# A graph layer's edge lists compacted in two parts, the first part ahead of the loop and the second inside it

## The chip, the cores and the metric

The kernel runs on one core of one Trainium2 chip. The metric is the device time of one execution in microseconds (us), the median of the runs of one kernel.

## The reference

The layer takes 6250 nodes of 128 features and 206250 edges sorted by destination. What it computes is this:

```python
h = relu(layernorm(x))                       # (6250, 128)
x_i, x_j = h[dst], h[src]
msg = concat([x_i, x_j - x_i], -1) @ W.T + b # per edge
out = segment_max(msg, dst, 6250)
x = x + where(isfinite(out), out, 0)
```

The message splits into a part of the destination (At, taken out of the maximum and added at the end) and a part of the source (Bt = h times the right half of W). So for each node the kernel needs the maximum of Bt rows over its edges.

## The kernel before

**Nodes and edges.** Each of the 128 partitions owns 49 destination nodes, and a window of 1792 edges (`WIN`) that holds all of them. Sources are split as 50 blocks of 125 (`q16` is the block, `swin - 125 * q16` the place in it). Two ways lead from an edge to the maximum:

- the **pair loop** handles, for every destination and every source block, at most one edge. For 13 tiles of up to 10 partitions (`tiles`) and 25 pairs of source blocks each (325 turns of the loop, `pairs`), the tensor engine spreads the chosen places (L739), the scalar engine makes a one-hot of them (L740), two matmul passes multiply it with Bt (L808), and the vector engine takes the maximum into `acc2` (L812, at the end of a tile L829).
- the **stream** handles the edges that are second or later of their (destination, block) cell. Each partition has a list of up to 512 (`REST`) of them. For every list position, GpSimd gathers one Bt row per partition by an indirect DMA (L98, 8 rows to a group, 6 group buffers `rows`), the vector engine runs a segmented maximum over it (L163), and a full group is stored to `M` (L167). A group buffer is free for the next gathers when its store has ended. Behind the last store, 49 gathers (`extract`, L98 again) fetch the row where each node's run ends.

**Everything is ordered by hand** (a manual schedule): each engine runs its instructions in the order in which the lines are reached. `due(k)` says how many stream rows are done after turn k of the loop.

**Before the loop** come, interleaved:

1. 27 `step()` calls: normalize, relu, weigh by W, store Bt and At (L547 to L584, on ACT, PE and SP). The gathers need all of Bt.
2. 46 tests (`shift`, `deep`, `off`, L491 to L505): for each edge, whether one of the 43 edges ahead of it in its run is in the same cell. The vector engine compares all 1792 columns, and the tensor engine adds the answers up in PSUM (`count`, L486).
3. `first` and `res` (L648 to L652): which edges go to the loop, which to the list.
4. Compaction of `res` to the front of each partition: a prefix sum (L666), packing (L675 to L678), and 11 `move`s, each a mask and a predicated copy over up to 1791 columns (L522, L523). `spread` makes from it the gather indices `ridx`, the destinations `sdl` and the limits `slim` (L526 to L534).
5. The first tile's one-hots (`onehots(0)`: `OHQ` by L203, its two end rows set by GpSimd in L200; `OHD` by L208), and its `products` (L246 to L262), from which the loop's first turn starts.

Of the kernel before, what the change touches and what calls it, by code (L numbers as in the profile page):

```python
# [29 lines left out]
F32 = mybir.dt.float32  # L30
# [20 lines left out]
REST = 512  # L51
SH = 43
# [10 lines left out]
def gnn_kernel(tc, x, src, dst, W, b, out):  # L63
# [23 lines left out]
    LASTD = N - (P - 1) * LD  # L87
    SPLIT = ((0, L // 16 * 16), (L // 16 * 16, L))
# [12 lines left out]
    with ExitStack() as ctx:  # L101
# [10 lines left out]
        with ExitStack() as body:  # L112
# [16 lines left out]
            ridx = keep.tile([P, REST], I32, name="ridx")  # L129
# [15 lines left out]
            def gather_group():  # L145
                i = state["gathered"]
                state["gathered"] = i + 1
                G = rows.tile([P, U, C], F32, name="G")
                Gt[i] = G
                for j in range(U):  # L150
                    k = i * U + j
                    gather(G[:, j], Bt[:, :], ridx[:, k:k + 1])
# [114 lines left out]
            with ExitStack() as pre:  # L267
# [68 lines left out]
                junk = pool.tile([P, WIN], BF16, name="junk")  # L336
# [8 lines left out]
                dwin = pool.tile([P, WIN], I32, name="dwin")  # L345
# [8 lines left out]

                kk = pool.tile([P, REST], F32, name="kk")

# [15 lines left out]
                def scales_a(g):  # L372
                    A_.activation(rstd[:, group(g)], mv[:, group(g), 1], AF.Sqrt, bias=eps)
# [29 lines left out]
                qa = pool.tile([P, W2], F32, name="qa")  # L403
# [38 lines left out]
                G_.iota(kk, pattern=[[1, REST]], base=1, channel_multiplier=0, allow_small_or_imprecise_dtypes=True)  # L442
# [35 lines left out]
                first = pool.tile([P, W2], BF16, name="first")  # L478
                val = pool.tile([P, W2], BF16, name="val")
                csum = pool.tile([P, W2], F16, name="csum")  # L480
                nres = pool.tile([P, 1], F32, name="nres")

                def count(e, s):
                    for c0 in range(0, W2, 512):
                        c1 = min(c0 + 512, W2)
                        T_.matmul(dup[:, c0:c1], identb, e[:, c0:c1], start=s == 1, stop=s == SH + 3)  # L486

                def shift(s):
                    e = work.tile([P, W2], BF16, name="eq")
                    i1 = KB[:, 65 - s:65 - s + W2] if s % 2 else KA[:, 64 - s:64 - s + W2]  # L490
                    V.tensor_tensor(e, KA[:, 64:], i1, ALU.is_equal)  # L491
                    count(e, s)

                def deep():

                    s = SH + 1
                    e = work.tile([P, W2], BF16, name="eq")
                    V.memset(e[:, :s], 0.0)
                    V.tensor_tensor(e[:, s:], dlc[:, s:], dlc[:, :W2 - s], ALU.is_equal)
                    count(e, s)  # L500

                def off(j, bound, op, s):

                    e = work.tile([P, W2], BF16, name="eq")
                    V.scalar_tensor_tensor(e, dlc, adj[:, j:j + 1], bound, op0=ALU.add, op1=op)  # L505
                    count(e, s)
# [13 lines left out]
                def move(i):  # L520
                    n = W2 - (1 << i)
                    V.tensor_scalar(sh_[:, :n], pk[:, 1 << i:], 1 << (19 + i), None, op0=ALU.bitwise_and)  # L522
                    V.copy_predicated(pk[:, :n], sh_[:, :n], pk[:, 1 << i:])  # L523

                def spread():
                    V.tensor_scalar(ridx, pk[:, :REST], 8191, None, op0=ALU.bitwise_and)  # L526
                    V.tensor_scalar(nres, csum[:, W2 - 1:W2], -1.0, float(W2), op0=ALU.mult, op1=ALU.add)
                    V.tensor_scalar(sh_[:, :REST], pk[:, :REST], 13, 63, op0=ALU.logical_shift_right,
                                    op1=ALU.bitwise_and)
                    V.tensor_scalar(kk, kk, nres, 63.0, op0=ALU.is_gt, op1=ALU.mult)  # L530
                    V.tensor_tensor(sdl, sh_[:, :REST], kk, ALU.max)
                    s = slim[:, 1:NS]
                    V.tensor_tensor(s, sdl[:, 1:NS], sdl[:, :NS - 1], ALU.is_equal)
                    V.tensor_scalar(s, s, -0.5, FMAX, op0=ALU.add, op1=ALU.mult)  # L534
# [3 lines left out]
                lw = ln.enter_context(tc.tile_pool(name="lw", bufs=2))  # L538
                st = {}
# [72 lines left out]
                for _ in range(6):  # L612
                    step()
# [11 lines left out]

                early = [(s, t, b0) for s, t in ((q16, TQ), (dlc, TD)) for b0 in range(0, NBLK, 4)]
                tests = [lambda s=s: shift(s) for s in range(1, SH + 1)]
                tests += [deep, lambda: off(0, LOb, ALU.is_lt, SH + 2), lambda: off(1, HIb, ALU.is_gt, SH + 3)]
                for n, f in enumerate(tests):
                    f()  # L630
                    if n in (4, 8):
                        load_x(5 + n // 8, (nc.sync, nc.sync))
                    if n % 8 == 5:
                        step()
                    elif n % 5 == 2 and early:
                        turned(*early.pop(0))
                    if n in (16, 32):
                        moments(3 + n // 32)
                        scales_a(3 + n // 32)
                    if n in (18, 34):  # L640
                        scales_b(3 + n // 32)
                assert not early
                cmp_.close()
                hots.append(hotx.enter_context(tc.tile_pool(name="hot0", bufs=1, side="right", reuse_waits="tile")))
                signs, vals = onehots(0)
# [5 lines left out]
                V.scalar_tensor_tensor(first, dup, 0.0, val, op0=ALU.is_equal, op1=ALU.mult)  # L651
                V.tensor_tensor(res, val, first, ALU.subtract)  # L652
                V.scalar_tensor_tensor(qa, q16, float(-L), swin, op0=ALU.mult, op1=ALU.add)
                V.scalar_tensor_tensor(val, qa, float(-L), first, op0=ALU.add, op1=ALU.mult)
                for n in range(2):
                    for f in signs[n * 12:n * 12 + 12]:
                        f()
                    step()
                for b0 in range(0, NBLK, 4):
                    turned(val, TV, b0)  # L660
                for g in (5, 6):
                    moments(g)
                    scales_a(g)

                V.tensor_scalar(first, res, -1.0, 1.0, op0=ALU.mult, op1=ALU.add)
                V.tensor_tensor_scan(csum, first, first, 0.0, op0=ALU.add, op1=ALU.max)  # L666
                for g in (5, 6):
                    scales_b(g)

                f_ = first[:, 1:]  # L670
                V.scalar_tensor_tensor(f_, dlf[:, 1:], 1.0, dlf[:, :WIN - 1], op0=ALU.mult, op1=ALU.is_lt,
                                       accum_out=badc[:, 0:1])
                V.scalar_tensor_tensor(f_, dlf[:, 1:], -1.0, dlf[:, :WIN - 1], op0=ALU.add, op1=ALU.is_gt,
                                       accum_out=badc[:, 2:3])
                V.scalar_tensor_tensor(pk, dlc, 8192.0, swin, op0=ALU.mult, op1=ALU.add)  # L675
                V.tensor_tensor(sh_, csum, res, ALU.mult)
                V.tensor_scalar(sh_, sh_, 19, None, op0=ALU.logical_shift_left)
                V.tensor_tensor(pk, pk, sh_, ALU.bitwise_or)  # L678
                for n in range(2):
                    for f in signs[24 + n * 13:37 + n * 13]:  # L680
                        f()
                    step()
# [3 lines left out]
                mats, rest = products(0, lambda: bank0)  # L686
                for f in mats:
                    f()
                for i in range(11):
                    move(i)  # L690
                    if made["ln"] < NH + 2:
                        step()
                    if 3 <= i < 7:
                        rest[i - 3]()
                while made["ln"] < NH + 2:
                    step()
                spread()
                ln.close()
                while state["gathered"] < 2:
                    gather_group()  # L700


                V.tensor_scalar(badc[:, 1:2], nres, float(REST), None, op0=ALU.is_gt)
# [17 lines left out]
            with ExitStack() as main:  # L721
                accp = main.enter_context(tc.tile_pool(name="accp", bufs=1, reuse_waits="tile"))
                acc = accp.tile([P, P * LD], F32, name="acc")
# [48 lines left out]
                def due(k):  # L772

                    return min(NS, int(2.05 * min(k, NP_) + 1.6 * max(k - NP_, 0)))
# [5 lines left out]
                for k, (t, i) in enumerate(pairs):  # L780
# [28 lines left out]
                    if i == 0:  # L809
                        V.tensor_copy(acc2[:, :, :n], ps[:, :, :n])  # L810
                    else:
                        V.tensor_tensor(acc2[:, :, :n], acc2[:, :, :n], ps[:, :, :n], ALU.max)  # L812
                    while state["ran"] < due(k + 1):
                        if state["gathered"] < NG and state["ran"] >= (state["gathered"] - GB + 1) * U:
                            gather_group()
                        stream_step()
# [122 lines left out]
```

## Time and profile before

| | |
|---|---|
| median of 10 runs (lowest, highest) | 920.14 us (917.55, 921.86) |
| the profiled execution, its own time | 922.75 us |
| its span, first to last instruction | 921.0 us |
| first gather of a Bt row | 180.28 us into the span |
| first turn of the loop reaches `acc2` (L810) | 181.12 us |
| first turn of tile 1, of tile 12 (L810) | 248.59 us, 810.26 us |
| last gather of a Bt row issued | 834.63 us |
| first and last gather from M | 844.53 us, 910.34 us |

Times inside the execution are counted from the start of the span; 1.75 us of the profiled time lie outside it. Busy time of an engine does not count its waits, register work and DMA issue.

### The profile page before, as it was taken

Reading aid. Unit: us, or ns where it says so; the run is one execution under the profiler, and the core shown is the slowest. Engines: PE = TensorE matmul, PEld = TensorE weight load, DVE = VectorE, ACT = ScalarE, POOL = GpSimd, SP = SyncE. Lnnn points to the kernel's source line nnn. Section 1 sums busy time; section 2 is a strip of 40 time slices with the busy share of each in tenths; the row PEclk is TensorE's granted clock in tenths of the full one; section 3 lists DMA queues with packets and bytes.
Section 4 is the critical chain, followed back from the end, with each engine's and each line's share of the span. In section 5 each row is a group of like instructions: output and inputs, shape, how many; then the busy total and the mean of one; then the engine's idle time right before and its main releaser. Section 6 shows DMA issues by size and latency. Waiting matters only on the chain.

```text
span 921.0 us, 14085 instructions
## 1 busy us (share of the span) xinstructions
PE 733.8 (80%) x4272; PEld 511.1 (55%) x4277; DVE 758.9 (82%) x1796; ACT 637.7 (69%) x1623; POOL 567.8 (62%) x638
## 2 busy tenths in 40 slices
PE   1799669868898989999989988999898979849310
PEld 0344345446576666766666666666666657637210
DVE  6689989688898988998989888998889898849532
ACT  0532665788897978998997989899888774626000
POOL 3400000177777777777777777777777777764774
PEclk9999755778999998999999999999999998978655
DMA  4760111322333333333333333333333323374532
GB/s 87 196 151 23 33 35 45 85 98 98 101 118 101 98 98 113 105 100 104 117 98 98 109 112 97 100 118 101 98 98 119 102 94 100 121 202 155 154 94 85
DMA packets 50455, 95.74 MB, mean 104 GB/s; under 512 B 12093, under 2 KB 31254, under 8 KB 50017
## 3 DMA queue, kind: packets, MB, share of 16 engines
q1 hardware_dynamic: 30628, 52.46, 17.1%
q0 software_dynamic: 18736, 41.84, 16.4%
q10 hardware_dynamic: 1009, 0.49, 0.3%
q8 instruction: 34, 0.56, 0.2%
q14 instruction: 48, 0.39, 0.1%
HBM read 50.05 MB, written 44.64 MB: 103 GB/s over the span
## 4 chain that ended last, share of the span: by engine, by line
POOL 26%; DMA 26%; PE 14%; DVE 14%; issue 14%; ACT 5%; POOLq 0%; ACTq 0%; DVEq 0%
POOL G L98 26%; DMA G<-Bt,ridx 23%; PE pm L562 4%; PE ps L808 3%; DVE acc L812 3%; DVE G L163 2%; DVE OHD L208 2%; PE dup L486 2%; DVE eq L491 2%; PE z L739 2%; DMA G<-M,last_e 2%; ACT oh L740 1%; PE pt L552 1%; ACT OHQ L203 1%; DVE stats L365 1%
## 5 line engine op out<-in xcount | busy, mean ns | idle before, releaser
L98 POOL DMA_INDIRECT G<-Bt,ridx x512 | 494.7, 966 | 238.8 <-issue 135.2
L808 PE MATMUL ps<-oh,Bp 126*128 126x490 f32 (+1 forms) x1300 | 409.0, 439 | 44.4 <-DVE acc L812 33.2
L740 ACT ACTIVATE oh<-z 126x490 fp32r<-126x490 f32 (+1 forms) x650 | 339.8, 584 | 116.9 <-PE z L739 115.8
L812 DVE TENSOR_TENSOR acc<-acc,ps 128x980 f32<-128x980 f32 (+1 forms) x312 | 359.7, 1153 | 18.1 <-PE ps L808 16.2
L808 PEld LDWEIGHTS ps<-oh,Bp 126*128 126x128 f32 x1300 | 252.0, 201 | 138.0 <-DVE acc L812 72.7
L163 DVE SCALAR_TENSOR_TENSOR G<-G,slim 128x128 f32<-128x128 f32 x511 | 177.8, 348 | 71.2 <-DMA G<-Bt,ridx 60.5
L739 PE MATMUL z<-Vf,Sel 114*126 114x490 f16 (+1 forms) x650 | 207.9, 394 | 26.2 <-ACT Vf L262 17.6
L203 ACT ACTIVATE OHQ<-TQ,sbias 128x140 bf16<-128x140 bf16 (+1 forms) x637 | 220.5, 428 | 0.0
L246 PEld LDWEIGHTS <-OHQ 128*51 128x51 bf16 x1792 | 96.8, 184 | 50.1 <-issue 49.8
L739 PEld LDWEIGHTS <-Sel 114*126 114x126 f16 x650 | 81.7, 141 | 46.4 <-issue 23.3
L246 PE MATMUL pv<-OHD,OHQ 128*51 128x13 bf16 (+5 forms) x1638 | 101.3, 241 | 3.8 <-DVE OHD L208 3.2
L208 DVE SCALAR_TENSOR_TENSOR OHD<-TD,TV 128x30 bf16<-128x30 bf16 (+5 forms) x637 | 87.9, 184 | 0.0
L98 POOL DMA_INDIRECT G<-M,last_e x48 | 51.2, 1066 | 23.3 <-issue 12.8
L562 PE MATMUL pm<-wT,hT 128*125 128x256 f32 x100 | 48.2, 583 | 20.2 <-ACT hT L556 20.2
L486 PE MATMUL dup<-eq,identb 128*128 128x512 bf16 (+1 forms) x179 | 40.6, 361 | 5.6 <-DVE eq L491 2.4
L863 PE MATMUL pf<-ident,acc 128*128 128x128 f32 x49 | 12.8, 431 | 33.7 <-DVE o L864 32.0
L562 PEld LDWEIGHTS pm<-wT,hT 128*125 128x125 f32 x100 | 23.1, 280 | 28.0 <-ACT hT L556 26.5
L749 ACT ACTIVATE dump<-sdl,nbias 128x512 bf16<-128x512 f32 x50 | 36.8, 736 | 0.1
L864 DVE TENSOR_TENSOR o<-G,pf 128x512 f32<-128x512 f32 x12 | 8.2, 687 | 33.1 <-DMA G<-M,last_e 33.1
L572 ACT CAST Bp<-pm 125x256 fp32r<-125x256 f32 x50 | 18.5, 370 | 23.0 <-PE pm L576 22.1
L200 POOL MEMSET OHQ<- 128x140 bf16 x4 | 0.8, 228 | 53.5 <-PE dup L486 53.5
L486 PEld LDWEIGHTS <-identb 128*128 128x128 bf16 x184 | 18.2, 100 | 23.9 <-issue 9.1
(199 smaller groups left out, 445.4 us busy)
## 6 DMA issues: line engine op xcount, KB each, us to landing
M<-G SPq DMA_DIRECT2D x64, 512.0 KB, 2.8
G<-Bt,ridx POOLq DMA_INDIRECT x512, 2.5
xa<-At SPq DMA_DIRECT2D x1, 2744.0 KB
G<-in_x SPq DMA_DIRECT2D x6, 448.0 KB, 4.4
Bt<-ba SPq DMA_DIRECT2D x12, 224.0 KB, 6.0
At<-ba SPq DMA_DIRECT2D x12, 224.0 KB, 2.9
xo<-in_x SPq DMA_DIRECT2D x3, 728.0 KB, 5.2
out_x<-o SPq DMA_DIRECT2D x3, 512.0 KB, 3.6
```

Source lines behind the costliest of these rows:

```text
L98: G_.indirect_dma_start(out=o, out_offset=None, in_=table, in_offset=bass.IndirectOffsetOnAxis(ap=idx, axis=0))
L163: V.scalar_tensor_tensor(G[:, j], state["prev"], slim[:, k:k + 1], G[:, j], op0=ALU.min, op1=ALU.max)
L203: A_.activation(oq[:, a, :, :nl], TQ[:, :, ls], AF.Sign, scale=2.0, bias=sbias[:, a:a + 1])
L208: V.scalar_tensor_tensor(o[:, bs_, :nl], TD[:, bs_, ls], float(d + 1), TV[:, bs_, ls], op0=ALU.is_equal, op1=ALU.mult)
L246: T_.matmul(o, oq[:, :, b_, l], r, start=k == 0 and b_ == 0, stop=b_ == NBLK - 1, skip_group_check=True)
L486: T_.matmul(dup[:, c0:c1], identb, e[:, c0:c1], start=s == 1, stop=s == SH + 3)
L562: T_.matmul(pm[:L, j], st["hT", i][:, j, :L], wT, start=j == 0, stop=False, skip_group_check=True)
L739: T_.matmul(z[:, :n], Sel[:, i + j], Vf[t % 2][:, :n], start=True, stop=True)
L740: A_.activation(oh[:, j, :n], z[:, :n], AF.Relu)
L749: A_.activation(dump, sdl, AF.Sign, scale=2.0, bias=nbias[:, c:c + 1], accum_out=ends[:, c:c + 1])
L808: T_.matmul(ps[:, j, :n], Bp[:, e, i + j], oh[:, j, :n], start=e == 0, stop=e == 1)
L812: V.tensor_tensor(acc2[:, :, :n], acc2[:, :, :n], ps[:, :, :n], ALU.max)
```

## The change

The edges are gone through in two parts. The tests run on the first 1024 columns alone, those are compacted, and the first 192 list rows are made of them; then the tests run on the other 768 columns. What remains of both (the first part's edges beyond 192 rows and all of the second part's) is packed before the loop, and its 11 moves and its `spread` are taken out one instruction at a time, one per turn of the loop's first 25 turns. Five groups of gathers (40 rows, before: two groups) stand ahead of the loop. `due` lets the stream run 20 rows ahead, with 2.4 rows per turn in tile 0 and 1.68 after it (before: 2.05 and 1.6). Two edge checks (`badc` columns 0 and 2) come earlier, `acc` is allocated early and lends its space to the work tiles.

```diff
+HALF = 1024
+REST0 = 192
...
+    K1 = REST - REST0
...
-            ridx = keep.tile([P, REST], I32, name="ridx")
+            ridx = [keep.tile([P, n], I32, name=f"ridx{i}") for i, n in enumerate((REST0, K1))]
...
-                for _ in range(6):
+                for _ in range(7):
                     step()
...
+                f_ = first[:, 1:]
+                V.scalar_tensor_tensor(f_, dlf[:, 1:], 1.0, dlf[:, :WIN - 1], op0=ALU.mult, op1=ALU.is_lt,
+                                       accum_out=badc[:, 0:1])
+                V.scalar_tensor_tensor(f_, dlf[:, 1:], -1.0, dlf[:, :WIN - 1], op0=ALU.add, op1=ALU.is_gt,
+                                       accum_out=badc[:, 2:3])
...
-                for n, f in enumerate(tests):
+                for n, f in enumerate(tests(0, HALF)):
                     f()
...
                     if n % 8 == 5:
                         step()
...
+                firsts(0, HALF)
+                step()
+                kept = work.tile([P, HALF], BF16, name="eq", bufs=4)
+                V.tensor_scalar(kept, res[:, :HALF], -1.0, 1.0, op0=ALU.mult, op1=ALU.add)
+                V.tensor_tensor_scan(csum[:, :HALF], kept, kept, 0.0, op0=ALU.add, op1=ALU.max)
+                step()
+                place(HALF, res)
+                moments(4)
+                scales_a(4)
+                step()
+                for i in range(10):
+                    for f in move(i, HALF, REST0):
+                        f()
...
+                    if i % 3 < 2:
+                        step()
...
+                V.tensor_scalar(ridx[0], sh_[:, :REST0], 8191, None, op0=ALU.bitwise_and)
...
+                limits(0, REST0)
+                moments(6)
+                scales_a(6)
+                for n, f in enumerate(tests(HALF, W2)):
+                    f()
+                    if n == 3:
+                        scales_b(6)
+                    if n % 6 == 1 and made["ln"] < NH + 2:
+                        step()
+                    elif n % 5 == 3 and early:
                         turned(*early.pop(0))
...
+                while state["gathered"] < GB - 1:
+                    gather_group()
                 cmp_.close()
                 hots.append(hotx.enter_context(tc.tile_pool(name="hot0", bufs=1, side="right", reuse_waits="tile")))
                 signs, vals = onehots(0)
...
+                firsts(HALF, W2)
...
                 V.tensor_scalar(first, res, -1.0, 1.0, op0=ALU.mult, op1=ALU.add)
                 V.tensor_tensor_scan(csum, first, first, 0.0, op0=ALU.add, op1=ALU.max)
...
+                place(W2, res)
                 for f in vals:
                     f()
                 bank0 = ps_m.tile([P, 512], F32, name="pm")
-                mats, rest = products(0, lambda: bank0)
-                for f in mats:
-                    f()
-                for i in range(11):
-                    move(i)
...
-                spread()
+                for fs in products(0, lambda: bank0):
+                    for f in fs:
+                        f()
...
+                later = [f for i in range(11) for f in move(i, W2, K1)]
+                later += [spread, spread2, lambda: limits(REST0, NS)]
                 ln.close()
-                while state["gathered"] < 2:
-                    gather_group()
...
-                    return min(NS, int(2.05 * min(k, NP_) + 1.6 * max(k - NP_, 0)))
+                    return min(NS, 20 + int(2.4 * min(k, NP_) + 1.68 * max(k - NP_, 0)))
...
                         V.tensor_tensor(acc2[:, :, :n], acc2[:, :, :n], ps[:, :, :n], ALU.max)
+                    if later:
+                        later.pop(0)()
                     while state["ran"] < due(k + 1):
                         if state["gathered"] < NG and state["ran"] >= (state["gathered"] - GB + 1) * U:
+                            assert state["gathered"] * U + U <= REST0 or not later
                             gather_group()
                         stream_step()
```

## The prediction

> **What bounds the kernel now.** The page's first two parts show no full engine (DVE 82%), but GpSimd's slices carry one flat level from the loop's start to its end:
>
> ```profile
> PE 733.8 (80%) x4272; PEld 511.1 (55%) x4277; DVE 758.9 (82%) x1796; ACT 637.7 (69%) x1623; POOL 567.8 (62%) x638
> ...
> POOL 3400000177777777777777777777777777764774
> ```
>
> A level of 7 could be a full engine, so I read GpSimd's timeline next, then the vector engine's for one late tile:
>
> ```profile
> 101.31 0.38 POOL L200 MEMSET OHQ<- 128x140 bf16 x2 [53.50 <-PE dup L486]
> 180.28 1.03 POOL L98 DMA_INDIRECT G<-Bt,ridx  x1 [78.59 <-ACT oh L740]
> ...
> 184.14 0.95 POOL L98 DMA_INDIRECT G<-Bt,ridx  x1 [0.30 <-issue]
> 185.39 0.94 POOL L98 DMA_INDIRECT G<-Bt,ridx  x1 [0.30 <-issue]
> ```
> ```profile
> 569.87 1.17 DVE L812 TENSOR_TENSOR acc<-acc,ps 128x980 f32<-128x980 f32 x1
> 573.10 0.74 DVE L163 SCALAR_TENSOR_TENSOR G<-G,slim 128x128 f32<-128x128 f32 x2 [2.07 <-DMA G<-Bt,ridx]
> ```
>
> A gather follows a gather at 1.25 us with only its issue gap between: GpSimd is full. The tile from 553.8 to 603.4 lasts 49.7 us, and all 4.9 us of vector idleness in it wait for gathers. So the loop's pace is 1.6 rows a turn at the gather pace (439 gathers from 249 to 807 us, 1.271 us each). Two stretches frame it: 180 us before the first gather (its releaser, named ACT, is the last Bt store, given out behind L569's copy at 176.53 and 0.59 us long), and at the end the 49 gathers from M:
>
> ```profile
> 840.51 12.79 DVE L812 TENSOR_TENSOR acc<-acc,ps 128x784 f32<-128x784 f32 x12
> ...
> 910.34 0.95 POOL L98 DMA_INDIRECT R<-M,last_e  x1 [0.30 <-issue]
> ```
>
> The last stream row ends at 840.6, twelve turns are left, the span ends 80 us later.
>
> **When the gathers start.** Vector work is the same to 38.7 us; the two edge checks (2.02 us each) bring it to 42.9. PE does seven steps (46.4, and 3.77 for one more) and begins the tests at 50.2. Per test PE streams 1024 columns; twelve L486 matmuls (5376 columns) took 2.43 us, so 0.46 us, 21.3 for 46; five steps between cost 1.6 to 2.0 us each. The vector tests cost 0.6 us (1.00 us for 1792 columns with some 0.07 fixed): PE ends about 83. Then, by the rows of 1792 columns scaled to 1024: `first`, `res` 1.8, prefix sum 2.6, packing 4.2, moments 2.1, ten moves 17.4 (3.4 us each at 1791 columns), moments 2.6, index work 2.8: `ridx[0]` stands at 117. Not the last wait: Bt needs all 27 steps. Two states of PE show in L562's pair of matmuls:
>
> ```profile
> 52.27 0.59 PE L562 MATMUL pm<-wT,hT 128*125 128x256 f32 x2
> ```
> ```profile
> 148.48 1.22 PE L562 MATMUL pm<-wT,hT 128*125 128x256 f32 x2 [0.47 <-ACT hT L556]
> ```
>
> The ten steps of the compaction stand alone on PE, as those at 141 to 160 us did, 3.77 us each: 85 to 124. The last four lie among the first twenty of the second tests; at the slow state 1.3 us for the first two tests and 3 for a step, then at the fast state 0.35 a test and 2 a step, with three transposes: the last copy at 144 to 145. The store took 3.2 us (177.1 to 180.28). First gather: **147**, 33 us earlier; 152 with PE slow throughout. The Trainium skill (TensorE: Matmul & The Clock Gate, What's actually happening) states that the clock doubles after some 3.4 us of sustained work; its rule would put the first gather at the 147. What it says beyond that no row here shows.
>
> Edits that cost nothing: GpSimd's counting row is 1024 long instead of 512 (L442 took 0.59 us, so some 0.5 more), in front of 53 us of idleness; the steps' stores go out earlier on SP, whose queue holds only the two late loads of x and the stores themselves until the stream's; the early `acc` is space alone.
>
> **When the loop starts.** In the program's order the memsets of `OHQ`'s end rows (L200) now stand behind the 40 gathers on GpSimd, and the first matmul of `products(0)` waits for them. 40 gathers are 50.1 us, so they end at 197; nothing is late next, since the vector work (second tests to 156, then 25 us to the last `vals`) ends about 181. Then 140 matmuls (126 took 6.87 us: 7.6), two copies 1.0, `diff` 1.84, the three activations 2.2, and from z to `acc2` 3.6 (177.55 to 181.12): first turn at **214**, against 181.1. The change frees GpSimd 33 us earlier and gives the 33 us back at the loop's start.
>
> **Tile 0.** It took 67.5 us, 54.8 of them vector work. Added: the moves (33.6 us from 135.35 to 168.93, 0.8 less by the narrower last ones), `spread` and limits 3.3, and 80 rows instead of 51 at 0.325 us (9.4). Sum 100, all on the vector engine, and `acc2` turns queue behind it, with PE and ACT (58 us busy) waiting. For 14 mask operations beside gathers no row exists: nearest is L385, 4.27 us beside GpSimd's memsets against 0.23 for the same form alone. Bounds: 0, and one gather each, 0.95 us, 13; I take 3, because gathers leave 0.3 us gaps. The Trainium skill (SBUF — State Buffer, Who interferes with whom) states that such operations and GpSimd's exclude each other for a whole instruction; by it alone tile 0 would take 113. Tile 0 ends at **317**, before: 248.6.
>
> GpSimd meanwhile: 48 gathers end at 208, then it needs a stored group (222), and from group 8 on each group waits for 8 stream rows, 12.9 us against the 10 it needs. 120 rows are gathered when tile 0 ends.
>
> **The stream to its end.** 392 gathers at 1.271 us are 498: from 319 to 817, last row about 821. `due` reaches 512 with turn 282, so 258 turns fit, 1.95 us each. Vector work per tile was 44.8 us; with 42 rows 45.5, 1.82 a turn; ACT's work in the shown tile was some 44.6. So the engines can follow, though not by much; I add 2 for two nearly full chains: **823**.
>
> **Behind it.** 42 turns are left, with neither stream nor signs. Twelve turns of 392 columns took 12.79 us; by columns 1.34 us for 490: 17 turns 23, remaining matmuls of `products(12)` and its activations 6, tile 12 27 and 5 at its head (806.5 to 811.3). That is 61, loop end 884. The 49 gathers from M run beside it (61 us, some 10 more while `xa` loads) and are hidden. Tail: the vector work after the loop, 8.1 us to the first output and 20.2 of maxima and sums (0.72 per L864, 1.23 per L869), then 7.2 from the last to the span's end: 36. Span 920, with the 1.75 us outside 921.7, against 922.75. The median of runs lies 2.6 below the profiled execution: **919.0**.
>
> So the start of gathering gains 33 us, the extraction's cover 31, and the late loop start, the moves in the loop and 30 more turns behind the stream take it back.
>
> **Rivals.** (1) Slower: the vector engine, not the gathers, sets the loop. If the mask operations lose a gather's time each (tile 0: 113) and turns don't get below the 2.0 us that tiles take now, 258 turns are 516, and the span is 214 + 113 + 516 + 61 + 36 = 940: 939 as a median. For it: ACT and PE were near 90% in every slice. Against it: the shown tile has no vector idleness but for gathers. It decides from 1.96 us a turn on.
> (2) Faster: PE fast through the last steps and second tests (gathers at 138), gathers at 1.2525 us (392: 491), 57 us behind the stream. 204 + 103 + 2 + 491 + 4 + 57 + 36 = 897: 896 as a median. For it: slices of PE's clock near full in 40 to 100 us; against it, the half clock of 104 to 160 us under the same step pattern.
> (3) The change doesn't do what it says: Bt, not the list, holds the gathers. If the steps drag on until the second tests end (156), gathers start at 160, the loop at 227, and the time is 932.
>
> **How the numbers follow.** A measurement of this kernel can tell 0.2% from no change (918.3 to 922.0). Likeliest case, 0.44: 919, own range 911 to 927; it lies on both sides (0.19 faster, 0.11 within, 0.14 slower). Slower by (1) 0.24 and (3) 0.11, faster by (2) 0.21. Together 0.40, 0.11, 0.49. The range takes in (3), (1) up to its middle and the upper half of (2), whose own unknowns are some 8 us either way, which leaves out about 0.10 above and 0.10 below: 901 to 939.
>
> **What would show it.** First gather near 147, released by a store; 40 gathers, then L213's memsets, then PE's first product within a microsecond; first turn near 214; tile 1's copy near 317; waits for gathers in the vector timeline only in the last tiles; last row about 823; no wait for gathers from M in the tail. Wrong if the products start before the 40th gather has gone, if tile 0 takes under 90 us, or if the vector engine waits for gathers from tile 2 on.

## The result, and the profile after

| | before | after |
|---|---|---|
| median of runs (lowest, highest) | 920.31 us (915.79, 922.58), 28 runs | 939.59 us (937.43, 941.67), 8 runs |
| profiled execution, its span | 922.75 us, 921.0 us | 937.92 us, 936.2 us |

The changed kernel is slower: the ratio is 1.0213, 95% interval 1.0200 to 1.0225. The forecast was 919.0 us, with a range up to 939. Some runs of the experiments below had a granted TensorE clock of 0.73 to 0.77 instead of the usual 0.86 to 0.91, and with it the kernel before took 1225 to 1254 us; to tell the theories apart, only the lengths of gathers are taken from these runs.

The steps of the prediction beside the trace of after:

| step | predicted | after |
|---|---|---|
| first gather of a Bt row | 147 us | 144.2 us |
| 40th gather has gone, L213's memsets | 197 | 204.3 |
| first turn | 214 | 219.8 |
| tile 0 ends (length) | 317 (103) | 321.8 (102.0) |
| rows gathered by then | 120 | 107 |
| last stream row | 823 | 837.8 |
| loop end | 884 | 900.2 |
| span | 920 | 936.2 |

From the last stream row to the end it takes 98.4 us, where 97 were forecast. So the miss lies in the stream, and it was there by the end of tile 0. First the page of after, parts 1 and 2, the rows that answer to those of before:

```profile
PE 736.2 (79%) x4274; PEld 517.7 (55%) x4277; DVE 794.5 (85%) x1883; ACT 637.4 (68%) x1623; POOL 593.8 (63%) x638
...
POOL 3500006873888777777777777777777777757570
```

GpSimd has the same 638 instructions as before and 26 us more busy time (593.8 against 567.8). Its slices, of about 23 us each, fill one place earlier (from the seventh instead of the eighth), but they hold 6, 8 and 7, a hole of 3 and three 8s before they come to the flat level of 7: the early stretch is not the pace that the prediction carried over. The gathers by stage, from the windows view of the gather's line (columns: window, its length, GpSimd's busy time in these gathers, their number, granted clock, DMA share, GB/s), after:

```profile
144.00:182.00 38.00, 31.22 (x22) 0.66 0.13 36
182.00:205.00 23.00, 16.99 (x18) 0.50 0.18 51
205.00:228.00 23.00, 7.61 (x9) 0.65 0.15 50
228.00:321.80 93.80, 76.12 (x59) 0.66 0.26 86
321.80:620.00 298.20, 226.59 (x236) 0.96 0.34 111
```

and the same view of before:

```profile
180.00:250.00 70.00, 52.87 (x55) 0.87 0.30 97
250.00:620.00 370.00, 281.16 (x291) 0.97 0.32 104
```

Busy time divided by number: 0.96 to 0.97 us a gather in both stages of before and 0.96 from tile 1 on in after, but 1.42 us in the first stage and 1.29 us in tile 0. With 0.945 us as the length of a gather alone, that is 10 us more ahead of the loop and 21 us more in tile 0. GpSimd's timeline of after shows which gathers:

```profile
144.24 1.04 POOL L101 DMA_INDIRECT G<-Bt,ridx  x1 [90.79 <-DMA At<-ba]
163.01 4.22 POOL L101 DMA_INDIRECT G<-Bt,ridx  x1 [0.30 <-issue]
203.39 0.94 POOL L101 DMA_INDIRECT G<-Bt,ridx  x1 [0.30 <-issue]
204.33 0.69 POOL L213 MEMSET OHQ<- 128x140 bf16 x4
...
227.96 0.94 POOL L101 DMA_INDIRECT G<-Bt,ridx  x1 [13.07 <-DVE G L176]
231.70 3.09 POOL L101 DMA_INDIRECT G<-Bt,ridx  x1 [0.30 <-issue]
```

and the vector engine's timeline at the same places shows what ran beside the two long ones:

```profile
162.59 3.89 DVE L742 TENSOR_TENSOR_SCAN acc<-acc 128x1792 f16<-128x1792 bf16 x1
231.45 2.29 DVE L547 COPY_PREDICATED acc<-acc 128x1791 int32<-128x1791 int32 x1
```

The gather of 163.01 ends at 167.23, 0.75 us behind the prefix sum's end; the one of 231.70 ends at 234.79, 1.05 us behind the predicated copy's. It looks as if a gather that is issued during such an instruction did its work only when that had ended. The vector instruction is not longer for it: this predicated copy took 2.29 us, and its twin of before, with no gather near, 2.33.

So the gathers begin 36.0 us earlier than before (144.24 against 180.28) and the last one is issued 1.1 us earlier (833.54 against 834.63). Of the 34.9 us between, 26.5 are longer gathers (521.2 us of busy time for 512, before 494.7) and 13.1 are the one wait for a group buffer at 227.96; some 5 us of waits near the end of before are gone.

In the tiles behind the first the vector engine waits for PE at first and for gathers later, as these lines of its timeline of after show (from tiles 2 and 9; the counterpart of before's pair at 570 us):

```profile
415.12 1.18 DVE L876 TENSOR_TENSOR acc<-acc,ps 128x980 f32<-128x980 f32 x1 [1.87 <-PE ps L872]
...
719.01 0.35 DVE L176 SCALAR_TENSOR_TENSOR G<-G,slim 128x128 f32<-128x128 f32 x1 [0.39 <-DMA G<-Bt,ridx]
```

From 322 to 620 us its waits for gathers sum to 0.6 us (tiles 1 to 6 take 47 to 50 us each), from 620 to 840 to 16.8 us (tiles 7 to 10: 51 to 54 us): there the stream has used up GpSimd's lead. And behind the last stream row, vector timeline, then GpSimd's:

```profile
838.47 2.50 DVE L876 TENSOR_TENSOR acc<-acc,ps 128x980 f32<-128x980 f32 x2 [0.64 <-PE ps L872]
...
879.26 20.32 DVE L876 TENSOR_TENSOR acc<-acc,ps 128x784 f32<-128x784 f32 x19
899.62 0.57 DVE L896 TENSOR_TENSOR acc<-acc 128x392 f32<-128x392 f32 x1
```
```profile
909.45 1.75 POOL L101 DMA_INDIRECT R<-M,last_e  x1 [0.30 <-DVE bad L935]
```

The loop goes on for 62 us behind the last row, and the last gather from M is issued 26.8 us before the end of the span (before: 10.7), so it is the turns that end last.

### The profile page after: what moved, and what is told of

It is laid out like the page before. It is cut to its first block, busy times and chain, and to the rows that moved or that the text cites. A ratio compares the mean times of both kernels' runs of the same rounds, so it can differ in the third digit from the quotient of the medians.

```text
span 936.2 us, 14221 instructions
## 1 busy us (share of the span) xinstructions
PE 736.2 (79%) x4274; PEld 517.7 (55%) x4277; DVE 794.5 (85%) x1883; ACT 637.4 (68%) x1623; POOL 593.8 (63%) x638
## 4 chain that ended last, share of the span: by engine, by line
PE 35%; DVE 22%; ACT 12%; POOL 11%; DMA 10%; issue 9%; ACTq 0%; DVEq 0%; SPq 0%; POOLq 0%
PE ps L872 13%; POOL G L101 11%; DMA G<-Bt,ridx 8%; PE z L803 7%; DVE acc L876 7%; ACT oh L804 5%; PE pv L259 4%; PE pm L581 4%; ACT OHQ L216 4%; DVE G L176 3%; PE dup L492 3%; DVE acc L547 2%; DVE OHD L221 2%; PE pt L571 1%; ACT dump L813 1%
## 5 line engine op out<-in xcount | busy, mean ns | idle before, releaser
L101 POOL DMA_INDIRECT G<-Bt,ridx x512 | 521.2, 1018 | 259.1 <-issue 140.3
L872 PE MATMUL ps<-oh,Bp 126*128 126x490 f32 (+1 forms) x1300 | 422.4, 450 | 47.1 <-DVE acc L876 39.6
L872 PEld LDWEIGHTS ps<-oh,Bp 126*128 126x128 f32 x1300 | 258.9, 205 | 135.4 <-DVE acc L876 63.9
L803 PE MATMUL z<-Vf,Sel 114*126 114x490 f16 (+1 forms) x650 | 212.1, 402 | 21.9 <-ACT Vf L275 14.0
L101 POOL DMA_INDIRECT G<-M,last_e x48 | 47.9, 998 | 26.7 <-issue 12.8
L581 PE MATMUL pm<-wT,hT 128*125 128x256 f32 x100 | 45.7, 556 | 13.6 <-ACT hT L575 13.6
L874 DVE COPY acc<-ps 128x980 f32<-128x980 f32 (+1 forms) x13 | 15.1, 1158 | 40.2 <-PE ps L872 40.1
L259 PE MATMUL pm<-OHD,OHQ 128*51 128x13 bf16 (+5 forms) x140 | 6.6, 238 | 43.7 <-POOL OHQ L213 43.7
L498 DVE TENSOR_TENSOR eq<-KA,KB 128x1024 bf16<-128x1024 int16 (+1 forms) x44 | 27.2, 618 | 14.9 <-PE dup L492 8.7
L547 DVE COPY_PREDICATED acc<-acc 128x1023 int32<-128x1023 int32 (+20 forms) x21 | 34.0, 1617 | 0.3
```

The lines of the kernel that those rows point to most:

```text
L101: G_.indirect_dma_start(out=o, out_offset=None, in_=table, in_offset=bass.IndirectOffsetOnAxis(ap=idx, axis=0))
L259: T_.matmul(o, oq[:, :, b_, l], r, start=k == 0 and b_ == 0, stop=b_ == NBLK - 1, skip_group_check=True)
L547: lambda: V.copy_predicated(pk[:, :n], sh_[:, :n], pk[:, 1 << i:n + (1 << i)])]
L581: T_.matmul(pm[:L, j], st["hT", i][:, j, :L], wT, start=j == 0, stop=False, skip_group_check=True)
L803: T_.matmul(z[:, :n], Sel[:, i + j], Vf[t % 2][:, :n], start=True, stop=True)
L872: T_.matmul(ps[:, j, :n], Bp[:, e, i + j], oh[:, j, :n], start=e == 0, stop=e == 1)
```

## The experiments

Two theories stood against each other. **A**: the gathers set when the last row comes, and vector instructions that run beside them, the moves above all, take GpSimd's time. **B**: the vector engine's long tile 0 and the 1.92 us that turns then take set the end, and longer gathers cost nothing.

**The moves' place taken by instructions that read PSUM.**

```diff
-                later = [f for i in range(11) for f in move(i, W2, K1)]
+                cur = {}
...
+                def again(m):
+                    for _ in range(m):
+                        V.tensor_tensor(cur["a"], cur["a"], cur["p"], ALU.max)
...
+                later = [lambda m=m: again(m) for i in range(10) for m in (1, 2)] + move(10, W2, K1)
...
+                    cur.update(a=acc2[:, :, :n], p=ps[:, :, :n])
```

> Edit: the first ten moves in tile 0 (20 instructions, 32.5 us of vector time) are left out; in their places the vector engine repeats the turn's own maximum of acc2 and the product in PSUM once or twice (30 x 1.16 us = 35 us). The second list stays unmoved, so its rows are of other edges. Tile 0 keeps its length on the vector engine, but these instructions have one input in PSUM. Theory A, the moves took GpSimd's time (gathers were 21 us longer in tile 0 than 0.945 us each): gathers in tile 0 go back to 0.95 us, about 16 more rows are gathered by its end, the last gather of the stream comes at about 814 instead of 833.5, the span is 936 less 16 to 20, so 916 to 920. Theory B, the vector engine's long tile 0 and its turns of 1.92 us set the end: the gathers may be early, but the last stream row stays at 834 to 838 and the span at 932 to 938.

Measured: 940.63 us (939.28 to 942.49; before in the same batch 921.82; ratio 1.021, 1.017 to 1.025). The lengthening of the gathers in tile 0 (the sum of what each took over 0.945 us) fell from 21.3 to 1.2 us, as A has it. But the last gather came at 831.2, only 2.3 us earlier: a repeat took 1.18 us, tile 0 became 108 us long, and GpSimd now waited 14.6 us more for group buffers. By its time it speaks for B, by its gathers for A, so the same was done with 25 repeats, which keep tile 0's length:

> Edit: as tile0_psum_reads, on the changed kernel itself (memsets behind the fifth group), but with 25 repeats of the maximum (30 us) for the ten moves instead of 30 (36 us), so that tile 0 lasts 102 us as in the changed kernel. It sizes what the 21 us of lengthened gathers cost there. If all of it counts: last stream gather 813, span 916 to 918. If most of it only takes the place of waits for a free buffer, which tile0_psum_reads had (15 us more of them): some 112 to 114 rows gathered when tile 0 ends at 322, last gather 826 to 829, span 929 to 932.

That run and two repeats (tile0_psum_reads_25b, tile0_psum_reads_25c) had the low clock (1309 to 1316 us); the fourth did not:

> The kernel of tile0_psum_reads_25, on a chip with the usual clock. If all of the 21 us of lengthened gathers counts in the changed kernel: last stream gather 813, span 916 to 918. If most of it only takes the place of waits for a free buffer: 112 to 114 rows gathered when tile 0 ends at 322, last gather 826 to 829, span 929 to 932.

Measured: tile 0 from 220.4 to 322.4, 102.0 us as in the changed kernel; 934.17 us (931.4 and 936.9; ratio 1.014, 1.005 to 1.023). Its gathers, the windows view for the stage from the wait to the end of tile 0:

```profile
228.80:322.40 93.60, 65.55 (x69) 0.65 0.29 93
```

0.95 us a gather, and 69 of them where the changed kernel has 59. At the end of tile 0 there are 117 rows, the last gather comes at 825.4 (8.1 us earlier), the last row 6 us earlier. So of the 20 us that the moves' place adds to gathers, 8 counted in the changed kernel. Another 8 stood where GpSimd would have waited for the stream to free a buffer (here 8.3 us in three waits beyond the first), and 4 came back behind tile 0, where gathers are 9.4 us longer in sum here and 5.7 in the changed kernel. Neither of the two expected spans was met: that of this execution is 935.1 us, only 1.1 below the changed kernel's, because behind the loop the vector engine waits 6.3 us for an output store (the longest such wait in the changed kernel: 1.2), which no run here explains.

**The loop's start and the turns behind the stream.** Two small edits, apart and together:

```diff
-                while state["gathered"] < GB - 1:
-                    gather_group()
+                gather_group()
                 cmp_.close()
                 hots.append(...)
                 signs, vals = onehots(0)
+                while state["gathered"] < GB - 1:
+                    gather_group()
...
-                    return min(NS, 20 + int(2.4 * min(k, NP_) + 1.68 * max(k - NP_, 0)))
+                    return min(NS, 20 + int(2.4 * min(k, NP_) + 1.6 * max(k - NP_, 0)))
```

> Edit: the four memsets of OHQ's end rows are issued behind the first group of gathers instead of behind the fifth. Theory A, the gathers run without a gap but for one wait and set the end: products(0) start when the vector work ends (182 instead of 205), the first turn comes at 197 to 199 instead of 219.8, the 13 us that GpSimd waited for a free group buffer go, the gathers stay lengthened by the vector work, last stream gather at 820, span 923. Theory B, the engines of the turns set the end: the whole 22 us come through, span 914. Theory C, the late loop start cost nothing: span 936.

Measured: 927.01 us (923.61 to 928.7; ratio 1.0059, 1.0037 to 1.0081), span 924.0. The first turn comes at 191.5, the wait for a buffer is gone, the last gather is at 818.9. The last gather and the span are A's to about a microsecond (820, 923), the first turn is 6 us earlier than A said. The loop's start moved by 28 us, the end by 12, since the gathers, now without a gap from 143.0 to 818.9, set it.

> Edit: due's slope after tile 0 is 1.6 rows a turn, as before the change, instead of 1.68; turn 295 instead of 282 brings the last row, so 30 turns instead of 42 lie behind the stream. Theory A, the gathers alone set when the last row comes: the last stream gather stays at 833 to 835, the loop ends 17 to 20 us earlier (882), and the gathers from M become the last work: span 919 to 922. Theory B, the engines need 1.9 us a turn from tile 0 on: turn 295 comes 24 us after turn 282, the last row at about 860, span 936 or more.

Measured: 925.81 us (924.64 to 927.77; ratio 1.0051, 1.0035 to 1.0067), span 924.0. The last gather stayed at 834.5 and the loop ended at 879 instead of 900, as A has it. The gathers from M (842.2 to 913.3) are last now; the span is 2 us above the range that A gave. B's last row at 860 did not come: turn 295 went with the last row, at 837.

> Edit: both of the two edits, the end rows' memsets behind the first group and the slope of 1.6. Theory A (gathers set the last row, 13 us of waiting gone, 30 turns behind): last stream gather at 820, gathers from M until 896, span 905 to 909, faster than before the change. Theory B (engines set the turns): first turn 198, turn 295 at 198 + 102 + 270 x 1.92 = 818, so nearly the same as A, 909 to 914; if the turns take 2.0 us as in the tiles before the change, 840 and a span of 925 to 930.

Measured: 911.53 us (910.23 to 912.77; ratio 0.990, 0.986 to 0.994), span 908.6, last gather 820.7, last gather from M 898.0. Against the changed kernel the two gains nearly add up (28.1 us together, 12.6 and 13.8 apart), and the kernel is faster than before the change. B's own number (909 to 914) lies so near that this run doesn't tell A from B by its time; only the gathers, which again have no gap, speak for A.

**Which vector instructions lengthen a gather.** On the kernel before, one kind of extra instruction in each of seven tiles.

```diff
+                def beside(t, a, p):
...
+                    if i // 2 % 3 == 1:
+                        beside(t, acc2[:, :, :n], ps[:, :, :n])
```

The condition holds in 8 turns of a tile; `beside` has the seven kinds.

> The kernel before, with extra vector work on scratch columns in 8 turns of each of the tiles 1 to 7, one kind to a tile: masks from SBUF into PSUM (tile 1, 16 of 490 columns), predicated copies within SBUF (2), masks within SBUF (3), two-input arithmetic within SBUF (4), the maximum with the product in PSUM once more (5), prefix sums with both inputs in SBUF (6), predicated copies with the mask in PSUM (7, 16 of 490). Theory A, an instruction that takes all of its inputs from SBUF holds up the gather beside it: by the rate of tile 0 (21 us more for 33 us of moves, 0.63 us for a microsecond) the gathers of tile 2 get longer by 6 to 7 us in sum, tile 3 by 3, tile 4 by 6, tile 6 by 10 or more, tile 5 by under 1; tiles 1 and 7 are not known: under 1 if a single SBUF input is harmless, 5 to 6 if any read of SBUF counts. Theory B, gathers get longer beside any busy vector engine: tiles 1, 5 and 7 as much as the others.

The one run had the low clock, and GpSimd was idle for a good part of each tile, so most sums are smaller than expected; the kinds stand apart all the same. Windows view of the gather's line, tiles 1 to 8 (tile 8 with nothing added):

```profile
327.00:399.60 72.60, 38.80 (x42) 0.76 0.22 74
399.60:470.90 71.30, 40.20 (x40) 0.79 0.22 74
470.90:550.80 79.90, 38.92 (x42) 0.76 0.20 67
550.80:622.10 71.30, 40.25 (x40) 0.81 0.22 74
622.10:702.00 79.90, 38.01 (x41) 0.77 0.20 66
702.00:764.60 62.60, 49.72 (x40) 0.89 0.26 84
764.60:842.90 78.30, 40.04 (x42) 0.72 0.21 69
842.90:927.10 84.20, 44.11 (x47) 0.78 0.21 69
```

Gather by gather over 0.945 us: predicated copies within SBUF (10.8 us of them) 3.3 us, two-input arithmetic within SBUF (9.7 us) 2.7, prefix sums (18.3 us) 12.2. Masks into PSUM (11.0 us) 0.2, the maximum out of PSUM (9.4 us) 0.7, predicated copies with the mask in PSUM (11.6 us) 0.9; the tiles with nothing added have 0.02 to 0.7. So Theory B's form of it, any busy vector engine, falls: two inputs from SBUF lengthen a gather, one from SBUF and one from PSUM does not. Of masks within SBUF (5.5 us) the sum, 0.8, tells too little.

The single gathers tell more, also that the kinds without effect did meet gathers. Of the gathers that began while an added instruction ran, 17 met one with PSUM on one side, and none of them took more than 0.95 us; 22 met one within SBUF, and 21 of them were longer (the other began 0.1 us before the instruction's end). Gathers that were under way when the instruction began took 0.94 to 0.95 us beside every kind, and the instruction was no longer for them: six of the eight prefix sums began beside such a gather, and all eight took 2.28 to 2.29 us.

A mask within SBUF holds a gather too, though it has one input. Three gathers that began during one took 1.02 to 1.13 us here; in tile 0 of the changed kernel nine took 1.28 to 1.77 us, and all twelve ended 0.81 to 0.82 us behind the mask. So in these runs it is an operand in PSUM that spares a gather, not the number of inputs. One pair of the changed kernel, and one with a mask into PSUM from kinds_beside_gathers, from their timelines:

```profile
235.87 1.09 DVE L545 TENSOR_SCALAR acc<-acc 128x1790 int32<-128x1790 int32 x1
236.34 1.44 POOL L101 DMA_INDIRECT G<-Bt,ridx  x1 [0.30 <-issue]
```
```profile
359.13 1.38 DVE L777 TENSOR_SCALAR ps<-acc 128x490 int32<-128x490 int32 x2
359.56 0.95 POOL L98 DMA_INDIRECT G<-Bt,ridx  x1 [0.30 <-issue]
```

**What the moves cost once no gather waits for a buffer.** early_psum_reads is end_rows_early with the 25 repeats in tile 0; its first run had the low clock (1316.1 us).

> The kernel of early_psum_reads again, on a chip with the usual clock. Theory A, once no gather waits for a group buffer, the 20 us that the moves add to gathers count in full: gathers of tile 0 lengthened by about 1 us in sum, last stream gather 800 instead of 818.9, span 905 instead of 924. Theory B, tile 0's rows on the vector engine set how far the gathers get, and GpSimd waits for buffers instead: last gather at 813 or later, span 918 or more.

Measured: 911.05 us (909.1 to 911.57; ratio 0.989, 0.987 to 0.992). Tile 0's stage in the windows view, end_rows_early first, then this kernel, both with a tile 0 of 102 us:

```profile
191.50:293.60 102.10, 82.05 (x66) 0.67 0.29 89
```
```profile
192.20:293.90 101.70, 77.08 (x81) 0.66 0.31 99
```

Fifteen more gathers in the same time, the last one at 801.8 instead of 818.9, the span 909.5 instead of 924.0. The gathers of tile 0 are 19 us shorter in sum, and 17 of them count for the last gather, so B's 813 or later did not come. The span is 14.5 us shorter, not the 19 that A gave, since here too the vector engine waits 6.3 us for an output store behind the loop.

**A version that uses it.** A move may keep its mask in the PSUM space that the tests leave free, but only ahead of the loop. So all that the first 25 turns took from the second list is run there, with one stream row behind each instruction, so that buffers come free.

```diff
-                    return [lambda: V.tensor_scalar(sh_[:, :n], ...), lambda: V.copy_predicated(pk[:, :n], sh_[:, :n], ...)]
+                    return [lambda: V.tensor_scalar(m[:, :n], ...), lambda: V.copy_predicated(pk[:, :n], m[:, :n], ...)]
...
-                later = [f for i in range(11) for f in move(i, W2, K1)]
+                later = [f for i in range(11) for f in move(i, W2, K1, dup.bitcast(I32))]
...
+                while later:
+                    later.pop(0)()
+                    stream_step()
```

It has the early memsets and a slope of 1.64, and one PSUM pool (ps_z) is allocated behind two others (ps_s and ps_v). moves_first_sbuf differs from it in one place: the masks stay in SBUF.

> Edit: on top of the early memsets, all that the loop's first turns took from the second list (11 moves, spread, limits) is run ahead of the loop, with one stream row behind each instruction and the masks written to the PSUM space of the tests instead of SBUF; due's slope 1.64. Theory A, masks out of PSUM spare the gathers: lengthening of the gathers 10 us as before the loop now, none by moves; the loop starts late, at 228 to 234, but tile 0 takes 66 to 70 us, so it ends at 297 as it did; last stream gather 798 to 803, turns at 1.92 us, span 890 to 898. Theory B, PSUM masks don't spare them or are slow: last gather at 815 or later, span 903 to 910.

> As moves_first_psum, but with the masks in SBUF as the changed kernel has them. Theory A: the loop starts 8 us earlier (a mask takes 1.1 instead of 1.9 us), gathers are lengthened by 30 us in sum as in the changed kernel, last stream gather 815 to 819, span 904 to 909. Theory B, the place of the masks is all the same to the gathers: last gather as in moves_first_psum, span the same or up to 8 us less.

Both had the low clock (1304.1 and 1306.2 us), but the lengthening of the gathers ahead of the loop showed: 10.8 us with the masks in PSUM, 34.1 with the masks in SBUF. Again, at the usual clock:

> The kernel of moves_first_psum again, on a chip with the usual clock. Theory A (gathers set the end, masks in PSUM spare them): first turn 234 to 236, tile 0 ends at about 300, lengthening of the gathers 11 us before the loop and under 2 in tile 0, one wait of some 6 us for a buffer, last stream gather 802 to 808, span 894 to 900. Theory B (tile 0's vector work and turns of 1.92 us set the end whatever GpSimd does): last row no earlier than in moves_first_sbuf_2, span 905 or more.

> The kernel of moves_first_sbuf again, on a chip with the usual clock. Theory A: first turn 222 to 226, tile 0 ends at about 290, gathers before the loop lengthened by 34 us, last stream gather 820 to 825, span 907 to 912. Theory B: 8 us less than moves_first_psum_2, since the masks are shorter.

Measured: 894.16 us (893.39 to 894.73) with PSUM, ratio 0.971, 0.969 to 0.974, and 923.58 us (915.07 to 927.39) with SBUF, ratio 1.0045, 1.0025 to 1.0065. The same place in both, GpSimd's timeline, PSUM first:

```profile
182.45 0.94 POOL L101 DMA_INDIRECT G<-Bt,ridx  x1 [0.30 <-issue]
183.69 0.94 POOL L101 DMA_INDIRECT G<-Bt,ridx  x1 [0.30 <-issue]
```
```profile
180.34 4.02 POOL L101 DMA_INDIRECT G<-Bt,ridx  x1 [0.30 <-issue]
184.67 3.43 POOL L101 DMA_INDIRECT G<-Bt,ridx  x1 [0.30 <-issue]
188.41 3.36 POOL L101 DMA_INDIRECT G<-Bt,ridx  x1 [0.30 <-issue]
192.07 6.15 POOL L101 DMA_INDIRECT G<-Bt,ridx  x1 [0.30 <-issue]
```

With SBUF masks a gather lasts as long as one move or two, and 36 rows are gathered when the loop starts at 223.4; with PSUM masks 61, when it starts at 231.6. Ahead of the loop the gathers are 34.1 us longer in sum with SBUF masks and 11.4 with PSUM masks. The last gather is at 802.4 against 822.7, the spans are 893.0 and 913.3. The loop that starts 8 us later ends 20 us earlier: what B expected is the wrong way round. The SBUF kernel's profiled execution is the fastest of its ten; most others are 7 us or more longer, and why is not settled, so of the 29 us between the medians only the 20 of the two traces are explained.

The kernel with the moves ahead of the loop and masks in PSUM is the fastest here, 2.9% below the kernel before and 4.8% below the changed one. That holds for the usual clock alone: at the low one it took 1304.1 us where the kernel before took 1253.6. In that trace GpSimd waits for group buffers in nearly every tile (one wait of 32.5 us at 244.4), so the gathers no longer set the pace there; what does was not tested.

## Why the prediction was wrong, and where it was right

**First gather, 147 against 144.2: right in sum, by terms that cancel.** Of the ten steps of the compaction eight took the 3.77 us (97.33 to 126.8). The first two, at 86.02 and 88.66, took 2.6, and then PE waited 6.49 us for ACT, and ACT for moments that the vector engine had not yet done; so the steps ended 3 us late. The last four took some 14 us where the prediction had 20. The two states are in PE's lines of after, one from the compaction and one from among the second tests:

```profile
97.33 1.22 PE L581 MATMUL pm<-wT,hT 128*125 128x256 f32 x2 [6.49 <-ACT hT L575]
...
132.35 0.59 PE L581 MATMUL pm<-wT,hT 128*125 128x256 f32 x2
```

Rival 3 (gathers at 160) falls with it.

**"40 gathers are 50.1 us": wrong, 60.1.** The order behind it was right: the memsets wait for the fortieth gather, PE for the memsets (its first product at 204.8), and nothing else was late, the vector work having ended at 181.6. But the prediction took the pace of gathers from inside the loop, where nearly all vector work reads PSUM or is short, and used it where the vector engine does prefix sums and arithmetic over 1792 columns within SBUF. These 10 us less the 2.8 of the earlier first gather, and some 1.5 less from the memsets to the first turn, are the 5.8 us by which the first turn was late.

**Tile 0, 103 against 102.0 us: right in sum, with the cost of contention on the wrong engine.** This is the step that failed. The prediction asked whether 14 mask operations lose time to gathers, bounded that by 0 and 13 us on the vector engine, and took 3. Measured: beside gathers a mask of 1790 columns took 1.09 us and a predicated copy 2.31, alone 1.09 and 2.26; no move in tile 0 was more than 0.2 us longer than one of the same columns alone. It never asked what GpSimd loses: its sum has that at nothing, without a reason. And it left the predicated copies out, which are twice as long as the masks. Measured: 21 us on GpSimd, of which 8 counted in the changed kernel. The 10 us of the step above are the same omission ahead of the loop.

The Trainium skill (SBUF — State Buffer, Who interferes with whom) says that the two exclude each other for a whole instruction and that the order of issue decides who waits, and it names, beside the fast modes, vector instructions with two SBUF inputs against GpSimd instructions that read SBUF. The runs agree with the second part, to the kind: prefix sums lengthened the gathers by 12.2 us, predicated copies with the mask in PSUM by under 1; masks within SBUF held them as well (1.28 to 1.77 us in tile 0). On the first part only one side showed: the gathers wait (4.02 instead of 0.945 us), but a vector instruction that began beside a running gather did not (2.28 us a prefix sum, with and without). No run here shows why. Used for the vector engine alone, as the prediction did, its 113 for tile 0 was 11 us too long.

**120 rows at the end of tile 0: wrong, 107.** Without the moves' contention there are 117 (tile0_psum_reads_25d), so ten of the thirteen missing rows are the moves', and the arithmetic of buffers and stream rows was good to 3. Thirteen rows at 1.27 us are 16.5 us; with tile 0's end 4.8 us late that is 21, and 7 came back: the remaining 405 rows took 516 us, where the prediction had 506 for 392.

**Turns at 1.95 us, 258 of them: near.** Tiles 1 to 6 took 47 to 50 us, 1.9 to 2.0 a turn, by PE and the vector engine, the late ones 51 to 54 by the gathers. Rival 1's time (939) came out by another way, so that is luck: its condition, slower mask operations and turns of 2.0 us throughout, did not hold. Rival 2's fast PE and gathers did not come.

**42 turns behind the stream, 61 us, and the tail of 36: right,** 62 and 36.0. The prediction had this cost in its sum, and slope_1_6 shows that it was avoidable: 13.8 us, since the gathers, not `due`, say when the last row comes.

**From span to median: 4 us.** The profiled execution of before was 2.6 us above its median, so 2.6 were taken off; that of after lies 1.7 below. Of the 20.6 us between forecast and median, 16.2 are the profiled execution's.

**Of the points that would have proved it wrong** none occurred before tile 6: the products did wait for the fortieth gather, tile 0 took over 90 us, and the vector engine waited 0.6 us for gathers up to 620 us. They guarded the order of events, not GpSimd's pace, which is where it failed.

## What to carry to other kernels

When work is moved beside the engine that bounds a kernel, ask what it does to that engine's instructions, not only how long it takes on its own: compare the mean duration of the bounding instruction stage by stage, and take a pace only from a stage with the same neighbours. For GpSimd's gathers the neighbours to look for are vector instructions with all of their operands in SBUF; a mask or an operand in PSUM spared them. An earlier start is worth only what the queue behind it can use: here it met 48 rows of buffers, a memset behind forty gathers, and a list of turns that had been sized for the old pace.

## What the runs showed of the hardware

- A gather that begins during one of the prefix sums, predicated copies, masks or two-input operations within SBUF ends about 0.75 to 1.05 us behind that instruction, so its length follows the neighbour's: 4.22 us beside a prefix sum of 3.89, 6.15 beside a row of moves. Gathers that were under way before the added instruction began took their 0.94 to 0.95 us. Back to back, moves let through one gather in 3.7 us instead of 1.25.
- The same mask costs 1.09 us into SBUF and 2.04 us into PSUM, the predicated copy after it 2.3 and 2.2 us (1790 columns). The dearer mask made the faster kernel.
- At a granted clock of 0.74 to 0.77 the kernel before took 1225 to 1254 us, and the changed forms lost more, not less (ratios 1.03 to 1.06). Both clocks are on record for one chip, chip 8 (0.89 and 0.76 for the kernel before), so the clock is no fixed property of a chip here.
